# Attention scores as 64 x 128 products instead of pairs of 64 x 64, and value products without the 256-column merge

## The chip, the cores and the metric

The kernel runs on one core of one Trainium2 chip. The metric is the device time of one execution in microseconds. A core has a matrix engine (TensorE, PE in the profile; its weight loads are a row of their own, PEld), a vector engine (VectorE, DVE), a scalar engine (ScalarE, ACT), GpSimd (POOL) and a queue engine (SyncE, SP) that here issues nearly all DMAs. TensorE multiplies a stationary block, which is loaded first, with moving columns that stream past it, and writes its sums into PSUM; the other engines read them from there. All data here is 32-bit floating point.

## The reference

A block of attention with 16 heads that share one set of keys and values, over 64 sequences of 128 tokens with 512 features, added to its input. Cut to what matters:

```python
xn = layernorm(x, g_in)                                   # x: (64, 128, 512)
q = (xn @ Wq).reshape(b, n, 16, 64).transpose(0, 2, 1, 3) * 64 ** -0.5
k, v = split(xn @ Wkv)                                    # 64 features each, shared by all heads
k, v = concat(null_k, k), concat(null_v, v)               # one more key ahead of the 128
sim = einsum('bhid,bjd->bhij', q, k) + concat(null_bias, attn_bias)
sim = where(causal or masked, -max, sim)
out = einsum('bhij,bjd->bhid', softmax(sim), v)
out = out.transpose(0, 2, 1, 3).reshape(b, n, 1024) @ Wo
return x + layernorm(out, g_out)
```

The change touches two of these steps: the scores `q k` and the sums of values `softmax(sim) v`.

## The kernel before

A batch is one sequence of 128 tokens. Four batches make a group (the q, k and v projections work by groups), two batches make a pair, and the main loop does one pair `d` per turn: `turn(d)` and then a body (`body_first` for d = 0, `body` up to d = 3, `body_full` from 4 to 29). The last two pairs have `turn_end` and `body_end`, and `turn_end(32)` with `body_last` closes. A turn computes the scores of pair `d` (batches a and b), then the values of pair `d - 1` (batches p and p + 1), whose softmax was made meanwhile. The body computes k, v and q of the following group, the output projection of pair `d - 1`, the layer norm and the store of pair `d - 2`. The q and output projections are made with seven products instead of eight (Strassen-Winograd), in the body twice over; their sums run on VectorE and GpSimd.

The order of the instructions on every engine is written out by hand: each engine executes its own instructions in the order of these calls, and waits only where a tile that it reads or overwrites is not ready. On TensorE a turn is: scores (a, first half), (b, first half), (a, second half), (b, second half), then values of p and of p + 1, then the keys and values of the next group (line 404), the q products (lines 603 and 697) and the output products (line 998).

Scores. The 128 query tokens of a batch are halved by `hf`. The first half only needs the first 64 keys (the mask is causal), the second half all 128. The 16 heads are arranged as 4 (`f`) by 2 (`r`) by 2 (`u`). `kT` holds the keys with their 64 features on partitions 0 to 63, and once more on 64 to 127, so `r` selects the rows of the array; `u` selects the columns, since the two heads of one `r` and `f` end on different partitions of the result. So the four products of an `f` use the four quarters of the array, each with a stationary block of 64 features by 64 tokens of q, and 64 or 128 keys as moving columns. In `qT` the two `u` of one token half lie next to each other. Results go to two PSUM tiles, one per `r`, and `scores_add` (VectorE, lines 795 and 797) adds the bias and mask to them, `scores_max` (line 802) takes the row maximum, `exps` (ScalarE, line 811) the exponential with its sum, `rinv` and `scale` (line 833, GpSimd) divide, and `blocks_T` (line 849) turns 32 x 32 blocks so that the keys lie on partitions.

Values. The keys on partitions come in four strips `s` of 32 rows. For each `s` and `r` the stationary block is 32 keys by 64 features of v (`vr`), the moving columns are 4 heads by 32 queries, 128 columns, for one block of queries, or 256 for two (`n`). So eight pieces of the array work next to each other. `turns` gives for each parity of `s` four steps with the key block `j`, the place of the first query block `to`, and `n`. The first step always has 256 columns. In the steady turns (3 < d < 30) `WIDE` merges the two steps of j = 1 for the strips s = 1 and 3 into one of 256 columns (for the second batch of even turns for s = 3 alone) and leaves out the step after it.

Which PSUM tiles are used is fixed: the values go to rooms "a", "w", "Y" and "w" (line 857), which ScalarE frees with four activations (`values_out`, line 930); the q product of line 603 takes room "a" next, the products of line 697 take "w".

Of the kernel before, what the change touches and what calls it, by code (L numbers as in the profile page):

```python
# [17 lines left out]
def kernel(  # L18
# [59 lines left out]
    nc = tc.nc  # L78
    B, N, DIM = x.shape
    H = attn_bias.shape[0]  # L80
    DH = w_kv.shape[1] // 2
# [8 lines left out]
    Q = 32  # L90
# [182 lines left out]
    xT, qT, vr = {}, {}, {}  # L273
# [117 lines left out]
    kT = hp.tile([P, NQ, GB, Q], FP, tag="kT", name="kT", bufs=1)  # L391
# [142 lines left out]
    def token_sum(g, k):  # L534

        xS[g, k] = gp.tile([P, GB // 2, HK, N], FP, tag=f"xS{k}", name=f"xS{k}_{g}", bufs=1)
        lo, hi = xT[g][:, 0 : GB // 2], xT[g][:, GB // 2 :]
        b11, b12 = lo[:, :, lo_k], hi[:, :, lo_k]
        b21, b22 = lo[:, :, hi_k], hi[:, :, hi_k]
        p, m = {  # L540
            1: (b12, b11),
            2: (b22, xS.get((g, 1))),
            3: (b22, b12),
            4: (b21, xS.get((g, 2))),
        }[k]
        nc.gpsimd.tensor_tensor(xS[g, k], p, m, ALU.subtract)
# [182 lines left out]
    def mask_neg(g):  # L729
        m8 = m8s.pop(g).rearrange("p (t j) -> p t j", t=GB)  # L730
        for keys, m in ((LK, m8[:, :, 0:NL]), (UK, m8)):
            nc.scalar.activation(
                mneg[:, :, keys], m, AF.Identity, bias=neg, scale=-NEG
            )
# [3 lines left out]
    def bias_add(b, parts=(slice(0, ROW),)):  # L738
        g, t = divmod(b, GB)
        if b < B - 1:  # L740
            S[b] = sp.tile([P, R8, ROW], FP, tag="s", name=f"s_{b}", bufs=3)
        else:
            S[b] = hp.tile([P, R8, ROW], FP, tag="xb", name=f"s_{b}", bufs=1)
        for keys in parts:
            nc.gpsimd.tensor_tensor(  # L745
                S[b][:, :, keys],
                biasp[:, :, keys],
                mneg[:, t, keys]
                .unsqueeze(1)
                .broadcast_to([P, R8, keys.stop - keys.start]),  # L750
                ALU.add,
            )
# [4 lines left out]
    def rooms(b, hf, tiles):  # L757

        nk = N if hf == 1 else NL
        return [  # L760
            pool.tile([P, NF, nk], FP, tag=tag, name=f"sc_{b}_{hf}_{tag}")
            for pool, tag in tiles
        ]

    def scores(b, hf, tiles=None):
        g, t = divmod(b, GB)
        nk = N if hf == 1 else NL
        if tiles is None:
            whole = ps_s.tile([P, 2, NF * nk], FP, tag="s", name=f"ps_{b}_{hf}")
            whole = whole.rearrange("p r (f j) -> p r f j", f=NF)  # L770
            home = [whole[:, r] for r in range(2)]
            pss[b, hf] = whole
        else:
            home = rooms(b, hf, tiles)
            pss[b, hf] = home
        for f in range(NF):
            for r in range(2):
                rows = slice(r * DH, (r + 1) * DH)
                for u in range(2):
                    nc.tensor.matmul(  # L780
                        home[r][u * DH : (u + 1) * DH, f, :],
                        qT[g, f // 2, t // 2][rows, f % 2, t % 2, hf, u],
                        kT[rows, 0 : nk // Q, t, :],
                        start=True,
                        stop=True,
                    )

    pss = {}

    def scores_add(b, hf):  # L790
        sv = S[b][:, :, KEYS[hf]].rearrange("p (r f) j -> p r f j", r=2)
        pv = pss.pop((b, hf))
        if isinstance(pv, list):
            for r in (1, 0):
                nc.vector.tensor_tensor(sv[:, r], pv[r], sv[:, r], ALU.add)  # L795
        else:
            nc.vector.tensor_tensor(sv, pv, sv, ALU.add)

    def scores_max(b, hf):
        if hf == 0:  # L800
            nmax[b] = small.tile([P, 2, R8], FP, tag="nmax", name=f"nmax_{b}")
        nc.vector.tensor_reduce(  # L802
            nmax[b][:, hf], S[b][:, :, WITH_NULL[hf]], AX.X, ALU.max, negate=True
        )

    def exps(b, hf, lo=0, hi=R8):
        if hf == 0 and lo == 0:
            rsum[b] = small.tile([P, 2, R8], FP, tag="rsum", name=f"rsum_{b}")
        for k in range(lo, hi):
            row = S[b][:, k, WITH_NULL[hf]]  # L810
            nc.scalar.activation(  # L811
                row,
                row,
                AF.Exp,
                bias=nmax[b][:, hf, k : k + 1],
                accum_out=rsum[b][:, hf, k : k + 1],
            )
# [38 lines left out]
    def values_rooms(  # L856
        p, rooms=((ps_q, "a"), (ps_w, "w"), (ps_y, "Y"), (ps_w, "w"))
    ):
        po = [
            pool.tile([P, 2, 2, NF, Q], FP, tag=tag, name=f"po_{p}_{s}")  # L860
            for s, (pool, tag) in enumerate(rooms)
        ]
        pos[p] = [t[:, :, 0] for t in po]
        pos[p + 1] = [t[:, :, 1] for t in po]
        return po
# [20 lines left out]
            ps_y.tile(shape, FP, tag="X", name=f"po_{p + 1}_3"),  # L886
        ]

    WIDE = (1, 3)

    def values(b, wide=()):

        g, t = divmod(b, GB)
        sb = sbs.pop(b)
        po = pos[b]
        turns = (
            ((0, 0, 2), (1, 1, 1), (2, 1, 1), (3, 1, 1)),
            ((0, 0, 2), (1, 0, 1), (1, 1, 1), (2, 1, 1)),
        )
        for turn in range(len(turns[0])):  # L900
            for s in range(NQ):
                j, to, n = turns[s % 2][turn]
                if s in wide and j == 1:
                    if turn == 2:
                        continue
                    n = 2
                quad = slice(s * Q, (s + 1) * Q)
                slots = slice(2 * to + j, 2 * to + j + 2 * n - 1, 2)
                for r in range(2):
                    rows = slice(r * DH, (r + 1) * DH)  # L910
                    nc.tensor.matmul(  # L911
                        po[s][rows, to : to + n],
                        vr[g][quad, t, PLACE[j], :],
                        sb[quad, slots, r * NF : (r + 1) * NF, :],
                        start=(turn == 0),
                        stop=True,
                        skip_group_check=(turn > 0),
                        tile_position=(s * Q, r * DH),
                    )
# [12 lines left out]
    def values_out(p, po):  # L932

        o = result_room(p)
        for s in range(NQ):
            u, i = divmod(s, 2)
            to = o[:, u].rearrange("p b f (s q) -> p s (b f) q", q=Q)[
                :, i : 4 - i : 3 - 2 * i
            ]
            add_null(to, po[s].rearrange("p s b f q -> p s (b f) q"), False)  # L940
# [148 lines left out]
    PAIRS = B // 2  # L1089
    late_T = []  # L1090

    def turn(d):

        a, b, p = 2 * d, 2 * d + 1, 2 * d - 2
        g = d // 2 + 1
        homes = (ps_y, "Y"), (ps_q, "a")
        if d == 1:
            homes = homes[::-1]
        scores(a, 0, (homes[0], (ps_w, "w")))
        scores(b, 0, (homes[1], (ps_w, "w")))  # L1100
        scores(a, 1)
        scores(b, 1, ((ps_y, "X"), (ps_q, "c")))
        scores_add(a, 0)
        scores_add(b, 0)
        scores_max(a, 0)
        scores_add(a, 1)
        scores_add(b, 1)
        po = values_rooms(p)
        steady = 3 < d < PAIRS - 2
        values(p, WIDE if steady else ())  # L1110
        values(p + 1, (WIDE if d % 2 else WIDE[1:]) if steady else ())
        if d % 2 and (d + 1) // 2 < NG:
            mask_neg((d + 1) // 2)
        bias_add(a + 2)
        if d % 2 == 0:
            token_sum(g, 1)
            token_sum(g, 2)
        exps(a, 0)
        values_out(p, po)

    def turn_end(d):

        a, b, p = 2 * d, 2 * d + 1, 2 * d - 2
        if d == PAIRS:
            blocks_T(*late_T.pop())
            late_nmr(p - 3)
            late_norm(p - 3)
            late_gain(p - 4)
            late_residual(p - 4, nc.gpsimd)
            values_rooms_apart(p)  # L1130
            result_room(p)
            for m in (p, p + 1):
                values(m)
                values_out_one(m)
            return
# [654 lines left out]
    for d in range(1, PAIRS - 2):  # L1790
        turn(d)
        (body_full if d > 3 else body)(d)
# [42 lines left out]
```

## Time and profile before

| what | value |
|---|---|
| median of 3 runs | 1023.64 us (1023.05 to 1023.94) |
| the profiled execution | 1022.45 us, its span 1020.6 us |
| TensorE matmul (PE) | busy 1012.9 us, 99% of the span |
| TensorE weight load (PEld) | busy 902.0 us, 88% |
| VectorE (DVE) | busy 860.8 us, 84% |
| GpSimd (POOL) | busy 775.0 us, 76% |
| ScalarE (ACT) | busy 672.8 us, 66% |
| DMA | 100.84 MB, mean 99 GB/s |

The span is the time from the first to the last instruction of the core in one execution; the time of that execution is a little longer, and the runs without a profile lie 0.6 to 1.5 us above it. A row of a group in the profile names the line of the kernel, the engine, the operation, the tile written and the tiles read, the shape (for products, rows by columns of the stationary block, then rows by moving columns), how often it occurs (x), the time in which at least one of them ran, the mean duration of one in ns, and the engine's idle time before them. Products overlap in the pipeline, so a duration is longer than the step from one to the next. A row of a window gives its bounds, its length, for each engine the busy time and the number of instructions that touch it, the granted TensorE clock as a share of full speed, the share of the DMA engines and GB/s.

### The profile page before, as it was taken

Reading aid. Unit: us, or ns where it says so; the run is one execution under the profiler, and the core shown is the slowest. Engines: PE = TensorE matmul, PEld = TensorE weight load, DVE = VectorE, ACT = ScalarE, POOL = GpSimd, SP = SyncE. Lnnn points to the kernel's source line nnn. Section 1 sums busy time; section 2 is a strip of 40 time slices with the busy share of each in tenths; the row PEclk is TensorE's granted clock in tenths of the full one; section 3 lists DMA queues with packets and bytes.
Section 4 is the critical chain, followed back from the end, with each engine's and each line's share of the span. In section 5 each row is a group of like instructions: output and inputs, shape, how many; then the busy total and the mean of one; then the engine's idle time right before and its main releaser. Section 6 shows DMA issues by size and latency. Waiting matters only on the chain.

```text
span 1020.6 us, 31143 instructions
## 1 busy us (share of the span) xinstructions
PE 1012.9 (99%) x12285; PEld 902.0 (88%) x12285; DVE 860.8 (84%) x1849; ACT 672.8 (66%) x2675; POOL 775.0 (76%) x621
## 2 busy tenths in 40 slices
PE   9999999999999999999999999999999999999997
PEld 9888888888888888888888888888888888888886
DVE  6877778888888988889888888888888888878787
ACT  5766677656677565686666776566765667856583
POOL 4997779678696876959768596785968769587686
PEclk9999999999999999999999999999999999999999
DMA  7415243151431425224152341514314152141221
GB/s 219 139 31 151 67 117 112 31 163 65 143 99 61 120 67 152 88 76 124 51 161 76 105 121 35 164 63 138 102 49 136 64 152 89 71 103 33 68 85 62
DMA packets 73833, 100.84 MB, mean 99 GB/s; under 512 B 32212, under 2 KB 36056, under 8 KB 71896
## 3 DMA queue, kind: packets, MB, share of 16 engines
q1 hardware_dynamic: 73392, 98.47, 32.3%
q8 instruction: 96, 1.57, 0.6%
q14 instruction: 49, 0.40, 0.1%
q10 hardware_dynamic: 296, 0.40, 0.1%
HBM read 63.19 MB, written 33.55 MB: 95 GB/s over the span
## 4 chain that ended last, share of the span: by engine, by line
PE 95%; ACT 2%; POOL 1%; DVE 1%; issue 0%; DMA 0%; POOLq 0%; DVEq 0%
PE pyX L998 20%; PE pa L603 13%; PE pi L697 11%; PE pyY L998 10%; PE po L911 8%; PE pkv L404 6%; PE pyw L998 5%; PE pc L603 4%; PE ps L780 3%; PE pq L499 3%; PE pa L554 2%; PE sc_X L780 2%; PE sc_Y L780 2%; PE pc L697 2%; ACT s L811 2%; PE pc L554 1%
## 5 line engine op out<-in xcount | busy, mean ns | idle before, releaser
L811 ACT ACTIVATE s<-s,nmax 128x65 f32<-128x65 f32 (+1 forms) x1024 | 370.9, 366 | 62.2 <-DVE nmax L802 62.2
L833 POOL TENSOR_TENSOR s<-s,rinv 128x512 f32<-128x512 f32 (+1 forms) x132 | 189.7, 1448 | 115.4 <-DVE rinv L829 112.9
L745 POOL TENSOR_TENSOR s<-biasp,mneg 128x1552 f32<-128x1552 f32 (+1 forms) x65 | 206.2, 3175 | 30.7 <-DVE s L795 21.2
L811 ACT ACTIVATION_READ_ACCUMULATOR s<-s,nmax 128x1 f32 x1024 | 194.5, 190 | 0.0
L725 DVE TENSOR_TENSOR qT<-pi,qT 128x128 f32<-128x128 f32 (+1 forms) x376 | 123.6, 340 | 35.9 <-PE pi L697 28.8
L1034 ACT COPY y<-pyX 128x256 f32<-128x256 f32 x29 | 10.8, 373 | 180.7 <-PE pyX L998 180.7
L802 DVE TENSOR_REDUCE nmax<-s 128x8 f32<-128x1032 f32 (+1 forms) x128 | 121.6, 950 | 0.1
L849 DVE STREAM_TRANSPOSE sb<-s 128x1536 f32<-128x1536 f32 (+1 forms) x68 | 113.6, 1674 | 2.1 <-POOL s L833 1.7
L998 PE MATMUL pyX<-wT,oT 128*128 128x256 f32 x464 | 109.7, 379 | 0.0
L998 PE MATMUL pyX<-wo,oT 128*128 128x256 f32 x464 | 109.7, 379 | 0.0
L978 POOL TENSOR_TENSOR oT<-oT 128x512 f32<-128x512 f32 x64 | 81.1, 1278 | 26.4 <-PE pyw L998 24.1
L998 PEld LDWEIGHTS pyX<-wT,oT 128*128 128x128 f32 x464 | 84.0, 190 | 9.2
L998 PEld LDWEIGHTS pyX<-wo,oT 128*128 128x128 f32 x464 | 84.0, 190 | 9.2
L911 PE MATMUL po<-sb,vr 32*64 32x128 f32 (+1 forms) x3700 | 86.2, 315 | 0.1
L911 PEld LDWEIGHTS po<-sb,vr 32*64 32x64 f32 x3700 | 74.8, 131 | 9.5 <-issue 5.3
L930 ACT ACTIVATE oT<-po,nv 128x512 f32<-128x512 f32 (+1 forms) x127 | 73.9, 660 | 0.4 <-PE po L911 0.4
L404 PE MATMUL pkv<-xT,wkv 128*128 128x256 f32 x256 | 63.3, 391 | 0.0
L998 PE MATMUL pyw<-wo,oT 128*128 128x256 f32 x256 | 60.5, 379 | 0.0
L998 PE MATMUL pyY<-wo,oT 128*128 128x256 f32 x256 | 60.5, 379 | 0.0
L998 PE MATMUL pyY<-wT,yS 128*128 128x256 f32 x256 | 60.5, 379 | 0.0
L614 ACT COPY qT<-pa 128x512 f32<-128x512 f32 x78 | 45.4, 582 | 17.7 <-PE pa L603 17.7
L404 PEld LDWEIGHTS pkv<-xT,wkv 128*128 128x128 f32 x256 | 46.2, 189 | 10.0 <-issue 4.8
(231 smaller groups left out, 2510.1 us busy)
## 6 DMA issues: line engine op xcount, KB each, us to landing
res<-in_x_dram SPq DMA_DIRECT2D x64, 256.0 KB
out_dram<-y SPq DMA_DIRECT2D x63, 256.0 KB
x<-in_x_dram SPq DMA_DIRECT2D x62, 256.0 KB
xd<-xb SPq DMA_DIRECT2D x14, 1024.0 KB
xT<-xd SPq DMA_DIRECT2D x56, 256.0 KB
vr<-vd SPq DMA_DIRECT2D x64, 128.0 KB
kT<-kT SPq DMA_DIRECT2D x32, 64.0 KB
vd<-vb SPq DMA_DIRECT2D x32, 64.0 KB
```

Of the source, the lines that this page charges most:

```text
L404: nc.tensor.matmul(pkv, wkv[:, kc, :], xT[g][:, t : t + 2, kc, :], start=(kc == 0), stop=(kc == KC - 1),)
L603: nc.tensor.matmul(prod[tag][:, i], w[:, kc, f * P : (f + 1) * P], t[:, :, kc, :], start=first, stop=(kc == HK - 1), skip_group_check=not ...
L697: nc.tensor.matmul(to, inner_w[k][i][:, h], inner_x[k, g][i], start=(i == 1), stop=True, skip_group_check=(i != 1),)
L725: nc.vector.tensor_tensor(o, p, o, ALU.add)
L745: nc.gpsimd.tensor_tensor(S[b][:, :, keys], biasp[:, :, keys], mneg[:, t, keys] .unsqueeze(1) .broadcast_to([P, R8, keys.stop - keys.start ...
L802: nc.vector.tensor_reduce(nmax[b][:, hf], S[b][:, :, WITH_NULL[hf]], AX.X, ALU.max, negate=True)
L811: nc.scalar.activation(row, row, AF.Exp, bias=nmax[b][:, hf, k : k + 1], accum_out=rsum[b][:, hf, k : k + 1],)
L833: nc.gpsimd.tensor_tensor(sv, sv, rinvs[b, hf][:, lo:hi].unsqueeze(2).broadcast_to([P, hi - lo, sv.shape[2]]), ALU.mult,)
L849: nc.vector.transpose(sbs[b][:, :, lo:hi].rearrange("p j e q -> p e j q"), S[b][:, lo:hi, 1 : ROW - 1].rearrange("p e (j k) -> p e j k", k=Q),
L911: nc.tensor.matmul(po[s][rows, to : to + n], vr[g][quad, t, PLACE[j], :], sb[quad, slots, r * NF : (r + 1) * NF, :], start=(turn == 0), st ...
L978: eng.tensor_tensor(o, a, b, op)
L998: nc.tensor.matmul(prod[key], h[:, c, :], w[:, c, :], start=(start and c == 0), stop=(c == HC - 1), skip_group_check=not start,)
```

## The change

In `scores` the loop over `u` goes: one product takes both heads as its stationary block, 64 features by 128 tokens (2 heads by 64), and writes all 128 partitions of the result; the rows (`r`), the moving columns and the results are the same. There are two products for each `f` instead of four. In `values` the merge is gone: each strip has the four steps of `turns` in all turns, and the two callers pass no `WIDE`. Nothing else changes, neither the order of the calls nor the tiles.

```diff
--- before.py
+++ after.py
@@ -776,14 +776,15 @@
         for f in range(NF):
             for r in range(2):
                 rows = slice(r * DH, (r + 1) * DH)
-                for u in range(2):
-                    nc.tensor.matmul(
-                        home[r][u * DH : (u + 1) * DH, f, :],
-                        qT[g, f // 2, t // 2][rows, f % 2, t % 2, hf, u],
-                        kT[rows, 0 : nk // Q, t, :],
-                        start=True,
-                        stop=True,
-                    )
+                nc.tensor.matmul(
+                    home[r][:, f, :],
+                    qT[g, f // 2, t // 2][rows, f % 2, t % 2, hf].rearrange(
+                        "p u i -> p (u i)"
+                    ),
+                    kT[rows, 0 : nk // Q, t, :],
+                    start=True,
+                    stop=True,
+                )
 
     pss = {}
 
@@ -886,9 +887,7 @@
             ps_y.tile(shape, FP, tag="X", name=f"po_{p + 1}_3"),
         ]
 
-    WIDE = (1, 3)
-
-    def values(b, wide=()):
+    def values(b):
 
         g, t = divmod(b, GB)
         sb = sbs.pop(b)
@@ -900,10 +899,6 @@
         for turn in range(len(turns[0])):
             for s in range(NQ):
                 j, to, n = turns[s % 2][turn]
-                if s in wide and j == 1:
-                    if turn == 2:
-                        continue
-                    n = 2
                 quad = slice(s * Q, (s + 1) * Q)
                 slots = slice(2 * to + j, 2 * to + j + 2 * n - 1, 2)
                 for r in range(2):
@@ -1106,9 +1101,8 @@
         scores_add(a, 1)
         scores_add(b, 1)
         po = values_rooms(p)
-        steady = 3 < d < PAIRS - 2
-        values(p, WIDE if steady else ())
-        values(p + 1, (WIDE if d % 2 else WIDE[1:]) if steady else ())
+        values(p)
+        values(p + 1)
         if d % 2 and (d + 1) // 2 < NG:
             mask_neg((d + 1) // 2)
         bias_add(a + 2)
```

## The prediction

> **What bounds the kernel now.** I read the page's busy times and its chain of waits first.
>
> ```profile
> span 1020.6 us, 31143 instructions
> PE 1012.9 (99%) x12285; PEld 902.0 (88%) x12285; DVE 860.8 (84%) x1849; ACT 672.8 (66%) x2675; POOL 775.0 (76%) x621
> ...
> PE 95%; ACT 2%; POOL 1%; DVE 1%; issue 0%; DMA 0%; POOLq 0%; DVEq 0%
> ```
>
> TensorE (PE) is busy for 99% of the span and carries 95% of the chain that ended last. So a microsecond added to its stream is a microsecond of the end, unless another engine was already being waited for, and none was. I therefore price the change on PE alone, by time from the first product of a stretch to the first product of the next, and look at the other engines only for new waits.
>
> The stretches that the change touches, by windows on PE: two of scores, then four of values. The first two of values have the wide form (an even and an odd turn), the last two, from early turns, don't:
>
> ```profile
> core 0: us, PE busy (x), PEclk, DMA share, GB/s
> 527.34:530.18 2.84, 2.84 (x129) 1.00 0.39 118
> 91.86:94.70 2.84, 2.84 (x130) 1.00 0.45 120
> 530.18:532.74 2.56, 2.56 (x120) 1.00 0.29 96
> 561.20:563.84 2.64, 2.64 (x117) 1.00 0.02 6
> 126.35:128.80 2.45, 2.45 (x132) 1.00 0.02 7
> 94.70:97.28 2.58, 2.58 (x132) 1.00 0.29 94
> ```
>
> Scores take 2.84 us early and late, at a granted clock of 1.00 throughout. One product of the code is two records in the trace (a turn's 64 score products are 128 records; what x has over that belongs to the neighbouring stretch).
>
> **The rounds inside the scores.** Four products, (r, u) = two halves of the rows by two halves of the columns, run side by side. First 64 keys, then 128 keys:
>
> ```profile
> 527.45 0.23 PE L780 MATMUL sc_Y<-kT,qT 64*64 64x64 f32 x2
> 527.51 0.23 PE L780 MATMUL sc_Y<-kT,qT 64*64 64x64 f32 x2
> ...
> 528.26 0.22 PE L780 MATMUL sc_a<-kT,qT 64*64 64x64 f32 x2
> ...
> 529.20 0.28 PE L780 MATMUL sc_X<-kT,qT 64*64 64x128 f32 x2
> ...
> 529.96 0.28 PE L780 MATMUL sc_X<-kT,qT 64*64 64x128 f32 x2
> ```
>
> The second round starts at 527.45 and the sixteenth at 528.26: 0.81/14 = 58 ns for a round of four records with 64 moving columns. With 128 columns, 0.76 us for seven steps: 109 ns. The ratio is not quite two, and both are close to the time of the moving columns alone.
>
> How many rounds there are:
>
> ```profile
> L780 PE MATMUL sc_w<-kT,qT 64*64 64x64 f32 x1024 | 37.1, 221 | 0.0
> L780 PE MATMUL sc_Y<-kT,qT 64*64 64x64 f32 x512 | 21.8, 224 | 0.1
> L780 PE MATMUL sc_a<-kT,qT 64*64 64x64 f32 x496 | 19.7, 218 | 0.0
> L780 PE MATMUL sc_X<-kT,qT 64*64 64x64 f32 x16 | 0.7, 224 | 0.0
> ```
>
> 1024 + 512 + 496 + 16 = 2048 records, in fours: 512 rounds of 64 columns. By the code the second halves (128 keys) are another 512.
>
> **What the change does to a round.** Two products instead of four: the same rows, the same moving columns, so the streaming time stays; the stationary block becomes 64 rows by 128 columns. So the question is how long a load of 128 columns takes. The trace never loads 64 rows by 128 columns; the nearest rows are these loads (PEld), each group just after a pause in which its buffers emptied, and the means of all:
>
> ```profile
> 496.26 0.14 PEld L780 LDWEIGHTS sc_Y<-kT,qT 64*64 64x64 f32 x2 [0.33 <-issue]
> 496.27 0.14 PEld L780 LDWEIGHTS sc_w<-kT,qT 64*64 64x64 f32 x2
> 496.31 0.14 PEld L780 LDWEIGHTS sc_Y<-kT,qT 64*64 64x64 f32 x2
> ...
> 532.74 0.19 PEld L404 LDWEIGHTS pkv<-xT,wkv 128*128 128x128 f32 x1 [0.17 <-issue]
> ...
> 532.85 0.41 PEld L404 LDWEIGHTS pkv<-xT,wkv 128*128 128x128 f32 x2
> ...
> L998 PEld LDWEIGHTS pyX<-wo,oT 128*128 128x128 f32 x464 | 84.0, 190 | 9.2
> L911 PEld LDWEIGHTS po<-sb,vr 32*64 32x64 f32 x3700 | 74.8, 131 | 9.5 <-issue 5.3 <-DVE s L795 0.8 <-DVE sb L849 0.6
> L780 PEld LDWEIGHTS sc_w<-kT,qT 64*64 64x64 f32 x1024 | 32.5, 134 | 0.0
> ```
>
> Of 64 columns the next load into the same place starts 0.05 us after the first (496.26, 496.31); of 128 columns 0.11 us after (532.74, 532.85). The mean durations say the same: 64 more columns cost 190 - 134 = 56 ns, while 32 or 64 rows make no difference (131, 134). A load depends on its columns, not on its rows. And loads of both row halves run at once today (sc_Y at 496.26, sc_w at 496.27, 10 ns apart), so I expect the two that are left to do so too.
>
> Today a round of 64 columns has loads (55) and streaming (55) about equal, hence 58. After it, loads take twice as long as the columns that stream past them, and the load sets the round. What a round of 128-column loads takes in a steady run:
>
> ```profile
> 18.57:22.14 3.57, 3.57 (x32) 1.00 0.45 113
> ```
>
> That is a run of 32 records of 128 by 128 with 128 moving columns: 3.57/32 = 111.6 ns. It is 2.6 ns over the 109 of the narrow loads, so there the load is the slower of the two. I take 111.6 ns for every round after the change; the lower end is the 0.108 us that two loads lie apart.
>
> By the Trainium skill, page "TensorE: Matmul & The Clock Gate", section "LDWEIGHTS (loading the stationary operand)", the time is the number of stationary columns over 1.2 GHz whatever the contraction: an estimate of 107 ns for 128 columns, 53 for 64. The trace agrees within 5 ns, and by the page alone the 512 rounds would cost 0.7 us less than at 108 ns (512 x 1.3 ns). It is a rule against this change, which halves the instructions but not the columns that are loaded. The page "TensorEngine Tiling (Array Packing)", section "Restrictions", says that tiling by columns turns off a fast weight load, which speaks for the change, since the new products no longer split the columns; by it the time would be that of rival 1. But the full-array f32 loads above aren't split either and take 0.11 us, so the trace doesn't bear it out for f32.
>
> **The sum for the scores.**
> - 512 rounds of 64 columns: 512 x (111.6 - 58.4) = +27.2 us (with 108: +25.4). The 58.4 is the 58 above, read to a tenth from the same records.
> - 512 rounds of 128 columns: 512 x (111.6 - 109) = +1.3 us (with the lower end, 0).
> - The first product of a stretch waits for its load: 108 instead of 55 ns. There are 35 stretches (2 before the loop, 29 turns, 2 in each of the last two turns): +1.9 us. The stagger of four starts falls to two, 14 ns each: -0.5 us.
> - Together +29.9 us; lower end +26.8.
>
> **The values.** The products with 256 columns at two places (slots of j = 1) become two of 128. The streamed columns stay, the records go from 116 or 112 to 128, and each of the eight tiles gets the same work in the same turn. The trace has this form already, in the turns before the wide one sets in: 2.45 us at 126.35, 2.58 at 94.70. The 2.45 is what streaming alone gives: two batches of 2 rounds of 218 ns (256 columns, twice 109) and 6 of 109 are 2.18 us, and a lead of 0.05, the stagger of eight starts and the drain make up the rest. In the 2.58 stretch the starts pause once for about 0.1 us with no semaphore there; I don't know why, and 2.58 is the upper end. Halving the score records gives the sequencer more time ahead of the values, which speaks for 2.45. The wide form is on in turns 4 to 29. 13 odd turns: 13 x (2.45 - 2.64) = -2.5; 13 even: 13 x (2.45 - 2.56) = -1.4; sum -3.9 us. At 2.58 everywhere: -0.8 + 0.3 = -0.5.
>
> **New waits.** Scores reach VectorE and ScalarE later, and the rooms of PSUM come free later:
>
> ```profile
> 528.78 0.41 DVE L795 TENSOR_TENSOR s<-sc_w,s 128x256 f32<-128x256 f32 x1
> ...
> 532.83 2.41 ACT L930 ACTIVATE oT<-po,nv 128x512 f32<-128x512 f32 x4
> ...
> 534.57 1.89 PE L603 MATMUL pa<-xT,wq 128*128 128x256 f32 x8
> ```
>
> Batch b's first half ends 16 rounds in: 0.91 us later than now, at about 529.43 instead of 528.5; its addition, queued at 528.78 today, moves by 0.66 us, and with it the maximum, the exponentials and the release of the first value room ("a", after the first of four activations, about 533.4, then 534.1). The q product that needs that room starts at 534.57 today; the scores of a turn grow by 0.93 (16 x 53 ns, 16 x 2.6, and the lead less the stagger), the values shrink by 0.11 to 0.19, so it moves to about 535.3. The slack stays near 1 us: no wait, price 0. If that cover were gone, the q products would stand behind ScalarE in every turn. No DMA is issued by any line changed, and PE's order is otherwise as before.
>
> **Total:** 29.9 - 3.9 = +26.0 us on the profiled execution's 1022.45 us (span 1020.6 and 1.85 around it) gives 1048.5. The median of the runs shown is 1.2 us above that execution, so 1049.7; I say 1049.5. The ends of the unknown prices give 26.8 - 3.9 = +22.9 (1046.6 against the median) and 29.9 - 0.5 = +29.4 (1053).
>
> **Rivals.**
> 1. *The load isn't the bound* (faster). If 64 rows by 128 columns load in the 55 ns of a 64 by 64 block, a round takes about 55.8 (half of 109 and a little) instead of 58.4: 512 x -2.6 = -1.3, stagger -0.5, values -3.9: 1018. It decides from a load of about 67 ns downwards, where 512 x (67 - 58.4) eats the 4.4 us gained elsewhere. For it: no row has this shape, and fewer rows could load faster. Against: 32 and 64 rows load alike, and 128 columns took twice 64.
> 2. *The two loads queue behind each other.* Then a round takes 2 x 108 = 216 ns: 512 x 157.6 + 512 x 107 = +135 us, with the rest of the sum about 1155. Against: four loads start within 20 ns today.
> 3. *A new wait.* The q product waits for the value room in each turn: up to 1 us more in 29 turns, about 1078. Against: the slack worked out above.
> 4. *Values don't speed up*: inside the range, 1053.
>
> **How the numbers follow.** Forecast (with 4) 0.81; rival 1 0.12; rival 2 0.03; rival 3 0.04. The forecast's own range is 1045 to 1054; for the whole 1040 to 1056, the lower side for rounds that lie between the two kinds of load, the upper for part of rival 3. Faster by over 0.2% (about what a measurement of this kernel tells from no change): rival 1, 0.12; within it 0.02 for a load near 67 ns; slower 0.86.
>
> **What would show it.** Score stretches of 3.77 us instead of 2.84; both kinds of round 111 ns apart; score loads of some 190 ns instead of 134; values 2.45 us in odd and even turns; PE still at 99% with no idle time before L603 and L404. Score rounds under 67 ns prove the forecast wrong, and values over 2.64 its smaller half.

## The result, and the profile after

| | before | after |
|---|---|---|
| median of 4 runs on one chip | 1023.39 us | 1048.53 us |
| lowest to highest | 1023.05 to 1023.94 | 1047.66 to 1049.21 |
| the profiled execution, its span | 1022.45, 1020.6 us | 1047.66, 1045.6 us |

The changed kernel is slower by 25.1 us, a ratio of 1.0246 (95% interval 1.0231 to 1.0261). The prediction was 1049.5 us, slower. The 4 runs before are the three of the table further up and one more.

The page of the kernel after, its busy times and its chain:

```profile
span 1045.6 us, 27775 instructions
...
PE 1037.4 (99%) x10601; PEld 929.1 (89%) x10601; DVE 863.8 (83%) x1849; ACT 675.8 (65%) x2675; POOL 775.0 (74%) x621
...
PE 95%; ACT 2%; POOL 1%; DVE 1%; issue 0%; DMA 0%; POOLq 0%; DVEq 0%
```

TensorE has 1684 records of products fewer and is busy 24.5 us longer. No other engine's busy time moved by more than 3.0 us, and the chain is split among the engines as it was. So the time was added on TensorE itself, and the end moved with it.

The windows of the kernel after, on PE (first the scores and the values of an even turn, then the values of an odd turn):

```profile
core 0: us, PE busy (x), PEclk, DMA share, GB/s
540.46:544.24 3.78, 3.78 (x66) 1.00 0.35 109
544.24:546.69 2.45, 2.45 (x131) 1.00 0.24 66
576.08:578.53 2.45, 2.45 (x130) 1.00 0.00 0
```

Scores went from 2.84 to 3.78 us with half the records, at the same granted clock; values from 2.56 and 2.64 to 2.45. Adding such stretches up over the whole execution, each from its first product to the first product that follows:

| all stretches, us | before | after | difference | predicted |
|---|---|---|---|---|
| scores | 91.51 | 121.29 | +29.78 | +29.9 |
| values | 84.16 | 79.29 | -4.87 | -3.9 |
| both | 175.67 | 200.58 | +24.91 | +26.0 |

That leaves 0.1 us of the span's 25.0 for everything else.

The timeline of the kernel after, PE's weight loads at the beginning of a score stretch, then its products (start, duration, engine, line, what):

```profile
540.46 0.18 PEld L779 LDWEIGHTS sc_Y<-kT,qT 64*128 64x128 f32 x1 [0.33 <-issue]
540.47 0.18 PEld L779 LDWEIGHTS sc_w<-kT,qT 64*128 64x128 f32 x1
540.57 0.19 PEld L779 LDWEIGHTS sc_Y<-kT,qT 64*128 64x128 f32 x1
540.58 0.19 PEld L779 LDWEIGHTS sc_w<-kT,qT 64*128 64x128 f32 x1
```

```profile
540.62 0.27 PE L779 MATMUL sc_Y<-kT,qT 64*128 64x64 f32 x1
...
540.74 0.27 PE L779 MATMUL sc_Y<-kT,qT 64*128 64x64 f32 x1
...
542.19 0.27 PE L779 MATMUL sc_a<-kT,qT 64*128 64x64 f32 x1
```

Both row halves load at once, 10 ns apart, and the next load into the same rows starts 0.11 us later. The products keep that step: from the second (540.62) to the sixteenth (542.19) of one row half 1.57/14 = 112 ns. A round takes 111.6 to 112 ns, with 64 moving columns as with 128. The Trainium skill, page "TensorE: Matmul & The Clock Gate", section "LDWEIGHTS (loading the stationary operand)", gives the time of a load as its columns over 1.2 GHz, an estimate of 107 ns for 128 columns; the steady round here is 5 ns above it.

The groups of the kernel after, kept apart by shape:

```profile
L779 PEld LDWEIGHTS sc_w<-kT,qT 64*128 64x128 f32 x512 | 59.5, 188 | 0.0
...
L779 PE MATMUL sc_w<-kT,qT 64*128 64x64 f32 x512 | 64.1, 275 | 0.0
```

The mean load is 188 ns against 134 before. The product's duration grew as well (275 against 221 ns) though the same 64 columns stream: I take it that the record includes the wait for the load, which is why the steps between starts, not the durations, are the thing to count.

No new wait: the waits of PE that the trace names after are the two of before (1.3 and 0.6 us, at the start and in the last output products) and one more of 0.5 us, ahead of transposes of the input (line 354). The timeline of the kernel after where the first value room comes free and is next needed:

```profile
546.69 1.99 PE L404 MATMUL pkv<-xT,wkv 128*128 128x256 f32 x8
546.74 2.42 ACT L925 ACTIVATE oT<-po,nv 128x512 f32<-128x512 f32 x4
...
548.52 1.67 PE L603 MATMUL pa<-xT,wq 128*128 128x256 f32 x7
```

Four activations in 2.42 us: the first ends near 547.35 (an estimate, a quarter of the 2.42), and the q product that needs its room starts at 548.52, 1.2 us later.

### The profile page after: what moved, and what is told of

The parts are those of the page before. It is cut to its first block, busy times and chain, and to the rows that moved or that the text cites. A ratio compares the mean times of both kernels' runs of the same rounds, so it can differ in the third digit from the quotient of the medians.

```text
span 1045.6 us, 27775 instructions
## 1 busy us (share of the span) xinstructions
PE 1037.4 (99%) x10601; PEld 929.1 (89%) x10601; DVE 863.8 (83%) x1849; ACT 675.8 (65%) x2675; POOL 775.0 (74%) x621
## 4 chain that ended last, share of the span: by engine, by line
PE 95%; ACT 2%; POOL 1%; DVE 1%; issue 0%; DMA 0%; POOLq 0%; DVEq 0%
PE pyX L993 19%; PE pa L603 13%; PE pi L697 10%; PE pyY L993 10%; PE po L906 7%; PE pkv L404 6%; PE pyw L993 5%; PE pc L603 4%; PE sc_Y L779 3%; PE ps L779 3%; PE pq L499 3%; PE sc_a L779 3%; PE sc_X L779 2%; PE pa L554 2%; PE pc L697 2%; ACT s L812 2%
## 5 line engine op out<-in xcount | busy, mean ns | idle before, releaser
L906 PE MATMUL po<-sb,vr 32*64 32x256 f32 (+1 forms) x4064 | 81.3, 300 | 0.1
L906 PEld LDWEIGHTS po<-sb,vr 32*64 32x64 f32 x4064 | 70.7, 130 | 7.1 <-DVE sb L850 0.6
L779 PE MATMUL sc_w<-kT,qT 64*128 64x64 f32 x512 | 64.1, 275 | 0.0
L779 PEld LDWEIGHTS sc_w<-kT,qT 64*128 64x128 f32 x512 | 59.5, 188 | 0.0
```

The costliest lines, as they stand in the source:

```text
L779: nc.tensor.matmul(home[r][:, f, :], qT[g, f // 2, t // 2][rows, f % 2, t % 2, hf].rearrange("p u i -> p (u i)"), kT[rows, 0 : nk // Q, t, :],
L906: nc.tensor.matmul(po[s][rows, to : to + n], vr[g][quad, t, PLACE[j], :], sb[quad, slots, r * NF : (r + 1) * NF, :], start=(turn == 0), st ...
```

## The experiments

Where a difference is given, the kernel before is the one that ran beside it on the same chip. No experiment leaves out any of the computation; two compute scores that are then not used.

**The two edits apart.** First the score edit alone, with the merged values of the kernel before:

```diff
     scores:  one product of 64 x 128 for both u        (as in the change)
     values:  WIDE and its callers as before
```

> The scores of the changed kernel (64 by 128), the values of the kernel before (with the merged 256-column step). Theory (the merged step itself costs TensorE its 0.1 to 0.2 us a turn): scores 3.77 us a turn as in the changed kernel, values 2.56 and 2.64 in steady turns as before, 2.45 in turn 2 and in the last two turns; 1023.4 + 29.8 - 1.2 = 1052.0 us. Rival (the values were slow before because 128 score records ahead of them emptied the queue): values 2.45 us, 1048.5 us, the same as the changed kernel.

Measured: 1051.59 us, 1.0277 (1.0263 to 1.029), +28.6 us. The windows on PE of this run, scores and values of an even turn:

```profile
478.65:482.42 3.77, 3.77 (x65) 1.00 0.37 112
482.42:484.98 2.56, 2.56 (x119) 1.00 0.24 66
```

The scores cost what they cost in the full change, and the merged values keep their 2.56. So inside the changed kernel the unmerged values are worth 1051.6 - 1048.5 = 3.1 us.

Then the value edit alone, with the four 64 x 64 score products of the kernel before:

```diff
     scores:  four products of 64 x 64 per f            (as before)
-        values(p, WIDE if steady else ())
-        values(p + 1, (WIDE if d % 2 else WIDE[1:]) if steady else ())
+        values(p)
+        values(p + 1)
```

> The scores of the kernel before (four products of 64 by 64), the values of the changed kernel. Theory: scores 2.84 us a turn, values 2.45 in steady turns, 2.9 and 3.1 in the last two turns as before: 13 x 0.19 + 13 x 0.11 = 3.9 us off, 1019.5 us, faster than both kernels. Rival (the queue runs empty after 128 score records, as in turn 2 of the kernel before): values 2.58 or more, 1022.9 us or slower.

Measured: 1030.65 us, 1.0077 (1.0064 to 1.009): **7.7 us slower** than the 1022.99 beside it, instead of 3.9 faster. My theory fell here, and the rival's side held. (The profiled execution, 1032.98 us, is one of the two longest of its six runs.) The windows on PE of this run, values of three turns:

```profile
188.85:191.30 2.45, 2.45 (x132) 1.00 0.02 7
219.75:223.24 3.49, 2.83 (x132) 1.00 0.26 80
784.16:788.00 3.84, 2.85 (x131) 1.00 0.20 62
```

The same 128 records take from 2.45 to 3.84 us. The timeline of this run inside the second of these, on PE's loads and on PE:

```profile
221.17 0.79 PEld L905 LDWEIGHTS po<-sb,vr 32*64 32x64 f32 x38
222.86 0.20 PEld L905 LDWEIGHTS po<-sb,vr 32*64 32x64 f32 x7 [0.91 <-issue]
...
220.93 1.27 PE L905 MATMUL po<-sb,vr 32*64 32x256 f32 x55
222.87 0.45 PE L905 MATMUL po<-sb,vr 32*64 32x128 f32 x7 [0.67 <-issue]
```

Everything stops, the loads for 0.91 us and the products for 0.67, and the trace names no semaphore ("issue"). So I counted the place of each pause in TensorE's stream of instructions, from the trace's records: two for a load and its product, one for a semaphore instruction. In 24 turns (21 of the 26 steady ones) the first product after a pause is number 195 or 196 of a run of 256, each time. What ran ahead of the first record isn't in that count, so place 195 may be the very border of a block. And the queue that the profile calls "instruction" moves packets of just this kind (page of this run, then of the kernel after):

```profile
q8 instruction: 99, 1.62, 0.7%
```

```profile
q8 instruction: 83, 1.36, 0.5%
```

1.62 MB in 99 packets is 16.4 KB a packet; single records say 16,384 bytes, which is 64 bytes for each of 256 instructions. In five pauses that I followed, the packet had landed 1.2 to 1.5 us before work resumed (221.61 and 222.86 in the case above). The other traces bear this out. Taken in order, there is one packet for each such place, and in none of the 1123 blocks of the twelve traces does TensorE go on there less than 1.2 us after the block's packet landed; the pauses of over 0.2 us inside scores and values end 1.2 to 1.6 us after it. The kernel before has little to spare: in its even steady turns that time is 1.4 to 2.1 us, without a pause. So I take the pause to be TensorE waiting for its own next instructions, though no run changed their supply alone. The Trainium skill, page "Runtime: NRT & Kernel Launch", section "Instruction fetch mechanics", describes such blocks of 256 instructions, fetched while the present one executes, and calls the cost of a border "mostly hidden". The blocks agree with this trace; "mostly hidden" doesn't where small products are dense (pauses in 24 turns, up to 1.4 us).

**Is it the load that sets the round?** In the changed kernel, and then in the kernel before, the first halves multiply all 128 keys instead of 64 (the 64 extra results aren't used): twice the moving columns with the same stationary blocks.

```diff
-        nk = N if hf == 1 else NL
+        nk = N
...
-                nc.vector.tensor_tensor(sv[:, r], pv[r], sv[:, r], ALU.add)
+                nc.vector.tensor_tensor(
+                    sv[:, r], pv[r][:, :, 0 : sv.shape[3]], sv[:, r], ALU.add
+                )
```

> The changed kernel, with all 128 keys as moving columns in the first halves too (the second 64 results aren't used). Theory (the load of 128 columns sets the round): rounds of the first halves stay at 112 ns with twice the moving columns, 1048.5 us within 1. Rival (the moving columns set the round): 512 rounds twice as long, + 512 x 56 ns = 29 us, 1077 us.

> The kernel before, with all 128 keys as moving columns in the first halves too. Theory (load and stream run side by side, and the longer sets the round): 512 rounds go from 58.4 to 109 ns, +25.9 us, 1049.3 us: what the change cost, without touching the shape. Rival (the number of records sets the round): as before, 1023.4 us.

Measured: with the wide blocks 1048.64 us, 1.0248 (1.0234 to 1.0261), the time of the changed kernel; with the narrow ones 1048.26 us, 1.0244 (1.0229 to 1.0258), which is +25 us over the kernel before. The windows of the scores on PE, of the wide and then of the narrow kernel:

```profile
541.12:544.89 3.77, 3.77 (x65) 1.00 0.37 109
```

```profile
540.24:543.90 3.66, 3.66 (x130) 1.00 0.39 117
```

This settles the mechanism. Under wide blocks, doubling the columns that stream costs nothing: all score stretches together take 121.29 us, as in the changed kernel. Under narrow blocks they go from 91.51 to 117.42 us, the 25.9 us of the expectation. Load and stream run side by side and the longer sets the round. The change made the load twice as long (0.11 instead of 0.05 us from load to load), and in the first halves only 64 columns stream past it.

**Only the second halves wide.** There the prediction saw almost no cost (109 to 111.6 ns). Unmerged values, and in `scores`:

```diff
+                if hf == 1:
+                    nc.tensor.matmul(home[r][:, f, :], ...)   # 64 x 128, as in the change
+                    continue
                 for u in range(2):
                     nc.tensor.matmul(                         # 64 x 64, as before
```

> The values of the changed kernel; scores of 64 by 128 for the second halves only (128 keys), the first halves with four products of 64 by 64. Theory (the load sets the round): rounds of the first halves 58 ns, of the second 111.6, scores 2.84 + 0.05 us and about 0.1 for the change of shape inside: 512 x 2.6 ns = 1.3 us, + 3 for the changes of shape, - 4 to - 5 for the values: 1022 to 1024 us, some pauses for instruction blocks on top (the turn isn't a multiple of 256). Rival (both halves share the loss): 1023 + 15 - 5 = 1033 us with scores 3.3 us a turn.

Measured: 1026.72 us, 1.0035 (1.0022 to 1.0048): above the theory's 1022 to 1024, well below the rival's 1033. The windows on PE, scores and values of a turn:

```profile
405.76:408.84 3.08, 3.08 (x97) 1.00 0.38 114
408.84:411.29 2.45, 2.45 (x130) 1.00 0.30 92
```

The rounds are what they should be, 58 and 112 ns, and the values are at 2.45 in 25 of 26 steady turns. What I hadn't priced is the change of shape in mid-stretch, by the timeline on PE:

```profile
406.69 0.23 PE L791 MATMUL sc_a<-kT,qT 64*64 64x64 f32 x2
406.70 0.22 PE L791 MATMUL sc_w<-kT,qT 64*64 64x64 f32 x2
406.86 0.71 PE L780 MATMUL ps<-kT,qT 64*128 64x128 f32 x8
```

The last narrow round starts at 406.69 and the first wide one at 406.86, 0.17 us later instead of 0.06; the second wide one follows after another 0.21 us instead of 0.11. So the change of shape costs about 0.2 us where I had put 0.1. Still, only 3.5 of the full change's 25 us are left, with the gain of the values in them. The scores alone add up to 99.84 us, 8.3 more than before, where the full change has 29.8 more: most of the loss lies in the first halves.

**Can the value edit be had without its pauses?** Two of the kernel before's turns are exactly 6 x 256 instructions long, so each steady turn meets the block borders at one of two places; the value edit alone makes it 1592, and the place drifts. If a fixed place is what keeps the kernel before free of pauses, padding to 7 x 256 should give 2.45 in all turns. The padding is increments of a semaphore that nobody waits for, on TensorE's queue, 40 after each of the first five output products of every other steady turn:

```diff
+    spare = nc.alloc_semaphore("spare")
+    def pad(k):
+        for _ in range(k):
+            nc.tensor.sem_inc(spare)
...
         out_product(p, 1, ps_y, "X")
+        pad(40 * h)
```

> The kernel of e2 (64 by 64 scores, no merged step), with 200 empty instructions on TensorE's queue in the body of every odd steady turn (increments of a semaphore nobody waits for, 40 after each of five output products), so that two turns are 1592 + 200 = 7 x 256 instructions. Theory (TensorE's instructions come in blocks of 256, and the next block isn't there in time where the block's end falls into the dense stretch; 256-instruction phases 153 and 184 at the first value product were without a pause): values 2.45 us in all steady turns, 1023.0 - 3.9 = 1019.1 us, faster than both kernels though it executes 2600 instructions more. Rival (the pauses come from something else, or from the number of instructions): 1030 us or more, as e2.

Measured: 1231.79 us, 1.2047 (1.2025 to 1.2069). As a time it's useless: the run is 208.6 us longer. In the trace, increments in a row start 151 ns apart, and the granted clock fell to 0.956 with TensorE busy for 87% of the span, so the 208.6 us aren't the increments alone. But the values, by windows on PE:

```profile
188.79:191.24 2.45, 2.45 (x133) 1.00 0.03 7
236.07:238.52 2.45, 2.45 (x132) 1.00 0.02 7
...
1124.61:1127.06 2.45, 2.45 (x132) 1.00 0.04 7
```

All 26 steady turns take 2.45 us, at their two fixed places. That fits the theory but doesn't prove it, since the increments also slow down what runs ahead of the scores, and so give the next block more time. That holds for every other turn; the 13 turns between, without increments in the body ahead of them, pass as well.

The cleaner test shifts the kernel before by 56 and by 16 places, once, in the first turn (`pad(28)` or `pad(8)` at two places of `body_first`).

> The kernel before with 56 empty instructions on TensorE's queue once, in the body of the first turn. All products, shapes and rooms as before. Theory: the phase at the first value product goes from 153 and 160 to 209 and 216 in every steady turn, where e2 paused 0.4 to 1.4 us: 26 turns x 0.3 to 1.3 us, 1031 to 1057 us. Rival: 56 x 51 ns at most once, 1023 to 1026 us.

> As e8 with 16 empty instructions: phases 169 and 176, which were without a pause in e2 (176, 177 and 184). Theory: no change, 1023.0 us within 0.2%. It also prices the empty instructions themselves.

Measured: shifted by 56, 1030.02 us, 1.0061 (1.0044 to 1.0078); by 16, 1022.91 us, 0.9998 (0.9989 to 1.0007). The first time lies between the theory's 1031 to 1057 and the rival's 1023 to 1026. In it, 4.9 us come with the increments (the scores of turn 1 start at 65.29 instead of 60.35), and the values of turn 2, which aren't merged, take 3.79 instead of 2.58 with a pause at place 195. The merged values stay at 2.56 and 2.63 at their new places, so they don't live by a lucky place. The shift isn't free for what stands around them: in two steady turns the scores take 3.06 and 3.01 us instead of 2.84 (from 347.10 and 533.88), and in four the first load of the keys behind the values comes late. From the first steady values to the last this is 1.4 us in all, against the 8 to 34 that the theory asks for. The theory of the fixed place is not borne out for the kernel before. Nor does the place alone decide in the value edit: there a turn at place 152 pauses (2.85 us, from 440.60), and one at 153 doesn't.

**One merge instead of two.** Only the first batch of a turn merged, and only the second (120 records a turn instead of 116 and 112):

```diff
         values(p, WIDE if steady else ())
-        values(p + 1, (WIDE if d % 2 else WIDE[1:]) if steady else ())
+        values(p + 1)
```

```diff
-        values(p, WIDE if steady else ())
-        values(p + 1, (WIDE if d % 2 else WIDE[1:]) if steady else ())
+        values(p)
+        values(p + 1, WIDE if steady else ())
```

> The kernel before, with the merged 256-column step in the strips 1 and 3 of the first batch of a pair only, in all steady turns; the second batch has four even steps. 120 value records a turn instead of 116 and 112. Theory (the merged step costs its time at the end, where the last strip runs alone, and an even second batch levels it out; the record count keeps the blocks of instructions in time): values near 2.45 us in steady turns, 1019.2 to 1020 us, faster than both kernels. Rival (120 records are too many for the blocks of 256): pauses at place 195 of a block as in e2, 1023 us or more.

> As e11, with the merged step in the second batch only: the same number of records, the same places of the blocks. Theory (the merge costs at the end): values 2.63 us in all steady turns, 1023.2 + 13 x 0.075 = 1024.2 us. Rival (each merge costs wherever it stands): values 2.54 us, 1021.7 us; with pauses both lie higher.

Measured: 1026.88 us, 1.0033 (1.0021 to 1.0044), and 1027.46 us, 1.0043 (1.003 to 1.0057). Both theories miss: turns without a pause take 2.56 and 2.60 us where I expected 2.45 and 2.63, and about 9 and 13 turns pause at place 195 or 196 again, up to 3.6 and 3.8 us. The first run's rival, pauses as in the value edit alone, held. A merge costs its 0.11 us in the first batch, 0.15 in the second; I suspect the order in which the eight pieces of the array start, but didn't test it.

How dense the instructions are, over the scores and values of a steady turn (a load or a product is one; the time without pauses), goes with the pauses of the values in these kernels, except for the padded one:

| kernel | instructions, time of the two stretches | time of 256 | steady turns with a pause |
|---|---|---|---|
| value edit alone | 512 in 5.3 us | 2.6 us | 21 of 26 |
| value edit alone, padded | 512 in 5.3 us | 2.6 us | none |
| merge in the second, first batch | 496 in 5.4 us | 2.8 us | about 13, about 9 |
| before | 488 or 480 in 5.4 to 5.5 us | 2.8 or 2.9 us | none |
| second halves wide, no merge | 448 in 5.5 us | 3.2 us | one |
| after | 384 in 6.2 us | 4.1 us | one, of 0.1 us |

No version that I ran beats the kernel before.

## Why the prediction was right, and where it was wrong

**The load sets the round: right.** Its step from 58.4 to 111.6 ns is 111.6 to 112 measured, and the two kernels with 128 keys show the cause, not only the size. The sum for scores was +29.9, measured +29.78. Rival 1 needed a load under 67 ns, rival 2 a round of 216; neither is there. The Trainium skill, page "TensorEngine Tiling (Array Packing)", section "Restrictions", says that splitting by columns turns off a fast weight load; for f32 nothing of that shows here, since the loads that aren't split take 188 ns against 134.

**No new wait: right.** The slack of about 1 us is 1.2, which leaves rival 3 nothing. But the sentence that no other engine was being waited for was not right: in the last two turns before, TensorE did wait for VectorE (below), and that wait went away.

**Values: right in sign and nearly in size, for a reason I had half.** The steady turns gave 13 x (2.45 - 2.56) + 13 x (2.45 - 2.64), but for one turn of 2.55, as the term said. The other 1.2 us I hadn't in the sum: unmerged turns that took more than 2.45 before. The windows of the kernel before, values of turns 30 and 31, and of the kernel after, the same two, with its one odd turn last:

```profile
964.01:966.90 2.89, 2.89 (x133) 1.00 0.03 6
982.36:985.45 3.09, 3.09 (x133) 1.00 0.26 82
```

```profile
989.07:991.52 2.45, 2.45 (x131) 1.00 0.00 0
1007.97:1010.42 2.45, 2.45 (x130) 1.00 0.42 105
353.11:355.66 2.55, 2.52 (x131) 1.00 0.29 105
```

In the first two, TensorE waited for a room that VectorE's addition of the scores had yet to free, by the timeline of the kernel before, on PE's loads:

```profile
964.56 2.16 PEld L911 LDWEIGHTS po<-sb,vr 32*64 32x64 f32 x116 [0.33 <-DVE s L795]
...
983.11 2.16 PEld L911 LDWEIGHTS po<-sb,vr 32*64 32x64 f32 x116 [0.46 <-DVE s L795]
```

After the change the stretches have no such wait. The two edits apart show which one took it away. With the score edit alone, values of the same two turns:

```profile
993.23:995.68 2.45, 2.45 (x131) 1.00 0.00 0
1012.11:1014.56 2.45, 2.45 (x130) 1.00 0.41 96
```

With the value edit alone they take 3.5 and 3.1 us (the first with a pause at place 195 or 196 as well). So it is the longer scores ahead, which give the addition its time. It makes 0.44 + 0.63, and turn 2 gave 0.13 (2.58 to 2.45), with the score edit alone as well: these 1.2 us, and not the 3.9, belong to the scores.

**The step that was wrong in its reasoning: "The trace has this form already, in the turns before the wide one sets in: 2.45 us".** I read a price of the unmerged form off turns 1 to 3 and booked the -3.9 to the value edit. But behind the scores of the kernel before, that price held in only 5 of the 26 steady turns. The edit alone costs 7.7 us, which I put down to 512 instructions that run past their supply. That the term came out near in the full change is in part luck: the other edit made room for it. The sentence "Halving the score records gives the sequencer more time ahead of the values" was the better ground, and I used it only to choose between 2.45 and 2.58. The pause in turn 2, of which I wrote "I don't know why", was the sign: it too resumes at place 195. I took 2.58 for the upper end of the form; the value edit alone shows 3.84.

So the two edits don't add up: +28.6 and +7.7 alone, +25.1 together, 11.2 less than the sum. As I read the pauses, the slow scores pay for the unmerged values by giving the instruction supply time, and they cost far more than they pay.

**The offset to the median** was put at 1.2 us and is 0.9 (1048.53 - 1047.66). Of the 1.0 us between 1049.5 and 1048.5, the two stretches make 1.1 and the offset 0.3; against them stand 0.3 us that the execution grew outside these stretches (0.1 of it in the span), and the 0.15 that the forecast was rounded down.

## What to carry to other kernels

Where a stationary block has more columns than stream past it (here 128 against 64, in 32-bit floating point), look at the load: it set the round, and joining blocks to halve the instructions took a round from 58 to 112 ns. Blocks side by side in the array loaded at the same time (starts 10 ns apart) and were the cheaper form for 64 moving columns; with 128 the two forms were 3 ns apart. Before you price an edit by the same form elsewhere in the trace, look at what runs ahead of it there: a dense stretch of small products, here 512 loads and products in 5.3 us, can pause for what looks like the supply of instructions: loads and products stop together, with "issue" as the releaser. Price edits that change the number of instructions together, not one by one.

## What the runs showed of the hardware that I had not expected

- TensorE seems to run out of instructions. With 512 loads and products in 5.3 us it pauses in 21 of 26 steady turns, up to 1.4 us, at the same place of 256, and goes on 1.2 to 1.6 us after the 16,384-byte packet landed; 488 in 5.4 us pass in the steady turns. Why the packet lands soon enough in some turns of the dense kernel (2.45 us at places 153, 176 and 184 of 256, for example), and in all of the padded one, isn't settled by these runs.
- Increments of a semaphore on TensorE's queue aren't free: in a row they start 151 ns apart (20 of them in the kernel shifted by 56). 56 in the first turn lengthened it by 4.9 us, while 16 there cost nothing that can be measured; 2600 made the run 208.6 us longer, part of it by a granted clock of 0.956.
- Going from 64 x 64 to 64 x 128 blocks in mid-stretch costs about 0.2 us, spread over the first two wide rounds.
- Unmerged and merged values differ by 0.11 to 0.15 us for one merged batch although the same columns stream; the cause stays open.
